# Scan decays, copies of B and small products in one ring of PSUM banks

## The chip, the cores and the metric

The kernel runs on one core of a Trainium2 chip. The metric is the device time of one execution in microseconds (us). The engines are named as in the profile: PE multiplies matrices (PEld is its loading of weights), DVE is the vector engine, ACT the scalar engine with the activation functions, POOL the GpSimd engine, and SP issues the DMAs. PSUM is the memory that PE writes its products to;[...] DVE and ACT read and write it too.

## The reference

Two layers work on four images of 48 x 48 tokens and 128 channels. The first normalises, projects, convolves (3 x 3, depthwise) and then runs a selective scan over the 2304 tokens in four directions `k` (by rows, by columns, and both reversed), for 256 channels with 16 states each:

```python
dt = softplus(dts + dt_proj_b)
A = -exp(A_logs).reshape(K, d, N)

def step(h, inp):
    dt_l, u_l, B_l, C_l = inp
    dA = exp(dt_l[..., None] * A)
    h = h * dA + (dt_l * u_l)[..., None] * B_l[:, :, None, :]
    y = einsum('bkdn,bkn->bkd', h, C_l)
    return h, y
```

The second layer is attention over the tokens, and then an STU: a causal convolution of the tokens with 16 spectral filters (`phi`), each followed by a projection with its own matrix, mixed over four lengths. Every layer adds to its input.

## The kernel before

**Stages.** The images follow one another. Each has a scan stage and then a stage of epilogue and attention. The scan stage runs beside matrix work that is independent of it: in image 0 `mixture` (products that mix the STU's matrices, into `gd` in DRAM), in images 1 to 3 the STU of the image before (`stu`). The STU of image 3 runs alone at the end.

**The scan stage.** A direction is cut into six chunks of `CS` = 384 tokens, so that an image has 24 chunks. A chunk has eight units `(h, q)`: a half `h` of the channels and a quarter `q` of the states. A unit works on a tile `s` of 128 partitions (32 channels by 4 states) by `G4` = 4 groups by 385 columns. Its life is:

- `spread` (L442): ACT copies the row of B, spread over the partitions (`bc`, in SBUF), into a PSUM bank (L445). Only for units whose multiply is on DVE.
- `enter` (L447): `s` = (dt u) times B in one multiply over 4 x 384 columns (L453). In three of eight units, the `POOLED` ones, POOL does it from `bc`; in five DVE does it from the copy.
- `decay` (L455), once for each group: ACT writes `exp(A dt)` (L459) into a PSUM bank `dA`. For group 0 it first copies the carried state into a spare column of `s` (L458).
- `scan` (L462), once for each group: DVE's `tensor_tensor_scan` (L465) runs over `s` with the decay as its factor.
- `times_c` (L468): POOL multiplies `s` by C (L474). `sum_c` (L476): PE sums the states into a bank `y` (L482). `add_y` (L485): DVE adds `y` to the image's sum (L488).

**Small products.** For the chunks ahead, `Chunk.prep` (L344) makes dt: a product `xp` (L370; only for `k` < 2, the other two directions read it from DRAM) that ACT copies to `xd` (L375), two products `dt` (L382) that ACT copies to `re` (L385), a softplus on ACT (L393), a multiply on DVE (L411), and a way through DRAM into the tiles `rep`, from which the units read. `prep` is a generator of three pieces for each unit's time. `mm_tile` hands its products a bank.

**The order of the work** is written out by hand in `scans` (L516), and each engine runs its own instructions in that order. Step `s` of its loop enters unit `s + 1` (POOL: `s + 2`), then takes the four scans of unit `s`, with a piece of `prep` before the first, before the third and after it; `spread(s + 2)` comes ahead of the third scan. Between the scans `more` advances the matrix work, by columns of PE's work, so that it ends with the scans. ACT's part of the matrix work falls between its decays: in `stu` a product `cx` (L1006) is copied to the bank `cy` (L1022), so that a second product may add to it, and then to `U` (L1029, L1030); the other one from `cy` to `U` (L1026). PE's next product on the same bank waits for these copies. In `mixture` they are the copies `Gm` (L829) and the scaled identities `W` (L839, L840).

**The PSUM banks of a scan stage**, eight in all: three for decays (`psa`; decay `i` takes bank `i` mod 3, and is issued just ahead of scan `i - 2`), one named B for the copies of B and the small products (`psB`), one for `y` (`psy`), two for `stu` or `mixture` (`psc`), one for the STU's projections (`psp`, which stays unused in image 0).

```python
        def scan(s, g):
            i = G4 * s + g
            decay(i + len(dAs) - 1)
            units[s].scan(g, dAs[i % len(dAs)])
```

Of the kernel before, what the change touches and what calls it, by code (L numbers as in the profile page):

```python
# [8 lines left out]
F32 = mybir.dt.float32  # L9
AF = mybir.ActivationFunctionType  # L10
ALU = mybir.AluOpType
AX = mybir.AxisListType
PSUM = bass.MemoryType.PSUM
DRAM = bass.MemoryType.DRAM

P = 128
B, H, W, C = 4, 48, 48, 128
# [4 lines left out]
CS = 384  # L22
SUB = 384
NT = L // P
G4, DL, C4, Q4 = 4, 32, 4, 4
# [30 lines left out]
def hybrid_kernel(ctx: ExitStack, tc: tile.TileContext, a: dict, out: bass.AP):  # L56
# [3 lines left out]
    nc = tc.nc  # L60
# [5 lines left out]
    bank = {}  # L66
# [246 lines left out]
    def in_order(t, k, lo, n):  # L313
# [2 lines left out]
            return t[:, lo // W:(lo + n) // W, :]  # L316
        return t.rearrange("p h w -> p w h")[:, lo // H:(lo + n) // H, :]

    def mm_tile(name):
        pool, tag = bank["mm"]  # L320
        return pool.tile([P, 512], F32, tag=tag, name=name)

    class Chunk:


        def __init__(self, b, k, c):
            self.b, self.k, self.lo = b, k, c * CS
            self.name = f"{b}_{k}_{c}"
            self.bc, self.rep = {}, []
            self.rev = k >= 2  # L330
            self.first = c == (NCH - 1 if self.rev else 0)
            self.last = c == (0 if self.rev else NCH - 1)

            self.slot = CS if self.rev else 0
            self.at = slice(0, CS) if self.rev else slice(1, CS + 1)

        def scanned(self, g):

            lo, n = g * (CS + 1), CS + 1
            if self.rev:  # L340
                return slice(lo + n - 1, lo - 1 if lo else None, -1)
            return slice(lo, lo + n)

        def prep(self, pool):  # L344

            k, name, xc = self.k, self.name, xcs[self.b]  # L350
            xdd_ = xdd[k % 2][self.lo // CS]

            def rest(n=1):

                yield
                yield 0
                yield
                for i in range(3 * n - 3):
                    yield 0 if i % 3 == 1 else None

            if k >= 2:
                xd = self.xd = pool.xd.tile([P, CS], F32, tag="xd", name=f"xd{name}")
                nc.sync.dma_start(xd, xdd_)
            yield from rest(2)
            yield
            if k < 2:
                xd = self.xd = pool.xd.tile([P, CS], F32, tag="xd", name=f"xd{name}")
                ps = mm_tile(f"xp{name}")
                for h in range(NH):
                    nc.tensor.matmul(ps[:, :CS], xw[:, h, k, :], in_order(xc[h], k, self.lo, CS),  # L370
                                     start=(h == 0), stop=(h == NH - 1))
            yield 2 * CS if k < 2 else 0
            yield
            if k < 2:
                nc.scalar.activation(xd, ps[:, :CS], AF.Identity, bias=onerow)  # L375
            yield from rest()

            re = pool.one.tile([P, NH, 2, CS], F32, tag="re", name=f"re{name}")
            for h in range(NH):
                yield  # L380
                ps = mm_tile(f"dt{name}_{h}")
                nc.tensor.matmul(ps[:, :CS], dtw[:, k, h * P:(h + 1) * P], xd, start=True, stop=True)  # L382
                yield CS
                yield
                nc.scalar.copy(re[:, h, 0], ps[:, :CS])  # L385
                if h == 0:
                    if k < 2:
                        nc.sync.dma_start(xdd_, xd)
                    yield from rest()
            yield  # L390
            yield 0

            nc.scalar.activation(re[:, :, 0], re[:, :, 0], AF.Softplus)  # L393
            yield
            yield
            yield 0
            d = dram.tile([NH, G4, DL, 2, CS], F32, tag="dtdu", name=f"dtdud{name}")

            def store(h):
                nc.sync.dma_start(d[h].rearrange("g j i t -> (g j) i t"), re[:, h])  # L400

            def load(h):
                rep = pool.rep.tile([P, G4, 2, CS], F32, tag="rep", name=f"rep{name}_{h}")
                for c in range(C4):
                    nc.sync.dma_start(rep[c::C4], d[h].rearrange("g j i t -> j g i t"))
                self.rep.append(rep)

            for h in range(NH):
                x = in_order(xc[h], k, self.lo, CS)
                dt, dx = [re[:, h, i].rearrange("p (r w) -> p r w", w=x.shape[2]) for i in range(2)]  # L410
                nc.vector.tensor_tensor(dx, dt, x, ALU.mult)  # L411
            yield
            yield
            store(0)
            yield 0
            store(1)
            yield
            yield from rest(2)
            load(0)
            yield from rest(2)  # L420
            yield
            yield 0
            load(1)
            yield
# [9 lines left out]
    class Unit:  # L434


        def __init__(self, ch, h, q):
            self.ch, self.h, self.q = ch, h, q
            self.name = f"{ch.name}_{h}_{q}"
            self.pool = (h, q) in POOLED  # L440

        def spread(self, ps):  # L442

            self.bt = ps.tile([P, 512], F32, tag="B", name=f"B{self.name}")
            nc.scalar.copy(self.bt[:, :CS], self.ch.bc[self.q])  # L445

        def enter(self, pool):  # L447

            full = self.full = pool.tile([P, G4, CS + 1], F32, tag="s", name=f"s{self.name}")
            s = self.s = full[:, :, self.ch.at]  # L450
            bt = self.ch.bc[self.q] if self.pool else self.bt[:, :CS]
            eng = nc.gpsimd if self.pool else nc.vector
            eng.tensor_tensor(s, self.ch.rep[self.h][:, :, 1], bt.unsqueeze(1).to_broadcast([P, G4, CS]), ALU.mult)  # L453

        def decay(self, g, dA):  # L455
            ch = self.ch
            if g == 0:
                nc.scalar.copy(self.full[:, :, ch.slot], none if ch.first else carry[:, self.h, self.q])  # L458
            nc.scalar.activation(dA[:, 1:CS + 1], ch.rep[self.h][:, g, 0], AF.Exp,  # L459
                                 scale=A[:, ch.k, self.h * G4 + g, self.q:self.q + 1])  # L460

        def scan(self, g, dA):  # L462
            ch = self.ch
            s = self.full.rearrange("p g t -> p (g t)")[:, ch.scanned(g)]
            nc.vector.tensor_tensor_scan(s, dA[:, CS + 1:0:-1] if ch.rev else dA[:, :CS + 1], s, 0.0,  # L465
                                         ALU.mult, ALU.add)

        def times_c(self):  # L468

# [43 lines left out]
            next(preps[2])  # L513
        yield chunks, preps

    def scans(b, chunks, preps, front, sp, back, work, work_cols):  # L516

        units = [Unit(ch, h, q) for ch in chunks for h, q in quads]
        total = len(chunks) * CHUNK_COLS + work_cols
# [10 lines left out]
        def enter(s):  # L530

            if s + 2 < len(units) and units[s + 2].pool:
                units[s + 2].enter(sp.s)
            if 0 <= s + 1 < len(units) and not units[s + 1].pool:
                units[s + 1].enter(sp.s)

        def decay(i):
            if i < G4 * len(units):
                units[i // G4].decay(i % G4, dAs[i % len(dAs)])

        def scan(s, g):
            i = G4 * s + g
            decay(i + len(dAs) - 1)
            units[s].scan(g, dAs[i % len(dAs)])

        def spread(s):
            if s < len(units) and not units[s].pool:
                units[s].spread(back.psB)

        def prepare(s):  # L550

# [10 lines left out]
                    nxt.fetch(i + u.q, front)  # L562

        pending = []
        dAs = [back.psa.tile([P, 512], F32, tag=f"dA{i}", name=f"dA{b}_{i}") for i in range(3)]
        for t in dAs:
            nc.vector.memset(t[:, 0:CS + 2:CS + 1], 0.0)
        spread(0)
        enter(-2)
        enter(-1)  # L570
        spread(1)
        for i in range(len(dAs) - 1):
            decay(i)
        for s in range(len(units) + 2):
            real = s < len(units)
            enter(s)
# [573 lines left out]
    def stu_alone(b, ps, seeds):  # L1150
        pool = Stage(tc, f"s{b}", "right", one=(1, SB), two=(2, SB), three=(3, SB), four=(4, SB))
        yield from stu(b, pool, ps, seeds)
        pool.close()
# [11 lines left out]
    start_y(0)  # L1165
    for b in range(B):
        sp = Stage(tc, f"h{b}", "left", s=(6, SB))
        ps = Stage(tc, f"b{b}", "right", psa=(1, PSUM), psy=(1, PSUM), psB=(1, PSUM), psc=(1, PSUM), psp=(1, PSUM))
        bank["mm"] = ps.psB, "B"
        if b == 0:  # L1170
            mixed = Stage(tc, "m", "right", two=(2, SB))
            scans(b, *first, front, sp, ps, mixture(mixed, ps), MIX_COLS)
            mixed.close()
        else:
            scans(b, *first, front, sp, ps, stu_alone(b - 1, ps, 1), STU_COLS)
        ps.close()
        sp.close()
        front.close()
# [20 lines left out]
        left = len(parts)  # L1199
# [75 lines left out]
```

## Time and profile before

| | |
|---|---|
| time, median of 3 runs | 5896.95 us (5894.11 to 5902.28) |
| profiled execution: its own time | 5896.91 us |
| its span, first to last instruction | 5895.2 us |
| granted PE clock, mean | 0.908 |
| scan stages, us from the span's start | 122 to 1092, 1382 to 2389, 2680 to 3682, 3973 to 4976 |
| a decay (L459), 3072 of them | 0.583 us |
| a scan (L465), 3072 | 0.942 us |
| a DVE multiply (L453), 480 | 1.734 us |
| a POOL multiply (L453), 288; (L474), 768 | 3.448 us; 3.178 us |

How to read it: a row of instructions gives line, engine, operation, `out<-in` by the program's names, the shape and the count, then the busy time in us and the mean in ns; after the second bar the idle time of the engine just before these instructions, and who ended most of it. A row of waits gives who waited for whom, then the total in us, how often, and the longest. A row of windows gives the stretch and its length, then for each engine the busy time and the number of instructions, the granted PE clock, the mean share of time that the DMA engines were busy, and GB/s. A row of the timeline gives start and length in us, engine, line, operation and names; in brackets the idle time before it and who ended it.

### The profile page before, as it was taken

The numbers are of one execution on the slowest core, as the hardware profiler recorded it, in microseconds if no ns is written. First come the engines' busy times: TensorE is split into PE (matmuls) and PEld (weight loads), VectorE is DVE, ScalarE is ACT, GpSimd is POOL, SyncE is SP. The second block draws the span as 40 slices with busy tenths as digits, with TensorE's granted clock in tenths as the row PEclk, the third lists the DMA queues.
The fourth block names the chain that finished last, engine by engine and source line by source line (L and its number), as shares of the span: only waits on it lengthen the run. The fifth ranks groups of instructions, "written<-read, shape, count | busy, mean of one in ns | idle before, by whom it ended". The sixth has DMA issues, their size and how long they took to land.

```text
span 5895.2 us, 74156 instructions
## 1 busy us (share of the span) xinstructions
PE 4906.8 (83%) x23826; PEld 3132.6 (53%) x23826; DVE 4268.4 (72%) x4926; ACT 3296.5 (56%) x6909; POOL 3620.1 (61%) x1823
## 2 busy tenths in 40 slices
PE   3555555597999998797999998779999998889999
PEld 1111111344566667545566666536666666468889
DVE  6999999756899998457999998548999997200000
ACT  2666666346777775246767765247777764332111
POOL 1999889504888998306888998107889987000000
PEclk6776777698999999898999999889999999999999
DMA  3444545206777778126877787127877876045546
GB/s 107 156 160 153 165 154 161 70 31 191 227 248 249 256 249 272 53 69 194 240 242 251 252 263 244 36 76 222 237 246 252 256 260 204 14 112 155 160 146 208
DMA packets 750565, 1066.87 MB, mean 181 GB/s; under 512 B 158528, under 2 KB 561088, under 8 KB 750144
## 3 DMA queue, kind: packets, MB, share of 16 engines
q1 hardware_dynamic: 744352, 1058.83, 57.6%
q10 hardware_dynamic: 5824, 3.30, 0.3%
q8 instruction: 190, 3.11, 0.2%
q14 instruction: 199, 1.63, 0.1%
HBM read 943.80 MB, written 117.98 MB: 180 GB/s over the span
## 4 chain that ended last, share of the span: by engine, by line
PE 45%; DVE 23%; DMA 11%; ACT 8%; POOL 5%; issue 4%; SPq 4%; ACTq 0%; DVEq 0%; POOLq 0%
PE cx L1006 15%; DVE s L465 11%; PE cy L1006 7%; PE pr L1069 5%; DVE s L453 5%; PE s L733 4%; PE y L482 4%; DMA rep<-dtdud 3%; PE o L726 3%; POOL s L474 3%; DMA tt<-fd 2%; SPq L432 2%; DVE xc L262 2%; ACT dA L459 2%; DMA bc<-xdd 2%
## 5 line engine op out<-in xcount | busy, mean ns | idle before, releaser
L465 DVE TENSOR_TENSOR_SCAN s<-dA,s 128x385 f32<-128x385 f32 x3072 | 2713.8, 942 | 217.6 <-ACT dA L459 216.5
L474 POOL TENSOR_TENSOR s<-s,bc 128x1536 f32<-128x1536 f32 x768 | 2438.9, 3178 | 131.6 <-DVE s L465 77.2
L459 ACT ACTIVATE dA<-rep,A 128x384 f32<-128x384 f32 x3072 | 1751.8, 583 | 801.0 <-DVE s L465 755.8
L453 POOL TENSOR_TENSOR s<-rep,bc 128x1536 f32<-128x1536 f32 x288 | 993.1, 3448 | 129.9 <-DMA bc<-xdd 119.6
L453 DVE TENSOR_TENSOR s<-rep,B 128x1536 f32<-128x1536 f32 x480 | 832.3, 1734 | 51.7 <-ACT B L445 26.2
L1006 PE MATMUL cx<-tt,us 128*128 128x254 f32 (+7 forms) x3840 | 815.4, 355 | 60.5 <-ACT U L1030 33.1
L1006 PE MATMUL cx<-tt,u 128*128 128x254 f32 (+7 forms) x3840 | 807.5, 353 | 48.4 <-ACT cy L1022 46.7
L1006 PE MATMUL cy<-tt,u 128*128 128x252 f32 (+5 forms) x3840 | 799.1, 352 | 39.8 <-DMA tt<-fd 39.8
L482 PE MATMUL y<-s,csum 128*32 128x384 f32 x6144 | 711.2, 537 | 140.2 <-POOL s L474 82.3
L1006 PEld LDWEIGHTS cx<-tt,u 128*128 128x128 f32 x3840 | 638.6, 190 | 295.7 <-issue 105.4
L1006 PEld LDWEIGHTS cx<-tt,us 128*128 128x128 f32 x3840 | 643.9, 192 | 255.8 <-issue 83.7
L1006 PEld LDWEIGHTS cy<-tt,u 128*128 128x128 f32 x3840 | 650.6, 193 | 187.8 <-issue 125.8
L1069 PE MATMUL pr<-U,G 128*128 128x288 f32 (+6 forms) x2048 | 593.2, 422 | 16.9 <-DMA G<-gd 16.7
L1096 DVE TENSOR_TENSOR res<-res,ot 126x512 f32<-126x512 f32 (+1 forms) x20 | 13.4, 671 | 687.1 <-PE ot L1090 687.1
L849 PE MATMUL G<-M,W 128*128 128x256 f32 (+3 forms) x512 | 244.4, 595 | 231.9 <-DMA M<-in_M_phi_plus 158.0
L1069 PEld LDWEIGHTS pr<-U,G 128*128 128x128 f32 x2048 | 342.8, 192 | 170.0 <-issue 94.9
L735 ACT ACTIVATE e<-s,shift 128x512 f32<-128x512 f32 (+1 forms) x360 | 230.8, 643 | 330.8 <-PE s L733 330.2
L156 POOL TENSOR_TENSOR ln_vu<-ln_vu,mhalf 128x4 f32<-128x4 f32 (+1 forms) x20 | 21.8, 1091 | 627.0 <-DVE ln_vu L155 627.0
L733 PE MATMUL s<-xnT 128*128 128x512 f32 (+1 forms) x720 | 357.2, 581 | 45.8 <-ACT xnT L695 23.3
L482 PEld LDWEIGHTS y<-s,csum 128*32 128x32 f32 x6144 | 126.9, 112 | 503.1 <-issue 286.6
L1029 ACT COPY U<-cx 128x252 f32<-128x252 f32 (+1 forms) x320 | 111.4, 348 | 420.3 <-PE cx L1006 420.1
L726 PE MATMUL o<-e,xn 128*128 128x512 f32 (+1 forms) x720 | 342.0, 558 | 4.5 <-ACT e L735 4.5
(161 smaller groups left out, 4016.4 us busy)
## 6 DMA issues: line engine op xcount, KB each, us to landing
rep<-dtdud SPq DMA_DIRECT2D x768, 384.0 KB
bc<-xdd SPq DMA_DIRECT2D x3072, 48.0 KB
tt<-fd SPq DMA_DIRECT2D x192, 577.0 KB
tt<-fd SPq DMA_DIRECT2D x192, 505.0 KB
dtdud<-re SPq DMA_DIRECT2D x192, 384.0 KB
tt<-fd SPq DMA_DIRECT2D x192, 379.0 KB
G<-gd SPq DMA_DIRECT2D x192, 256.0 KB
tt<-fd SPq DMA_DIRECT2D x64, 506.0 KB
```

The lines of the kernel that those rows point to most:

```text
L262: nc.vector.scalar_tensor_tensor(xc[h], x, cw[:, h, t:t + 1], xc[h], ALU.mult, ALU.add)
L453: eng.tensor_tensor(s, self.ch.rep[self.h][:, :, 1], bt.unsqueeze(1).to_broadcast([P, G4, CS]), ALU.mult)
L459: nc.scalar.activation(dA[:, 1:CS + 1], ch.rep[self.h][:, g, 0], AF.Exp, scale=A[:, ch.k, self.h * G4 + g, self.q:self.q + 1])
L465: nc.vector.tensor_tensor_scan(s, dA[:, CS + 1:0:-1] if ch.rev else dA[:, :CS + 1], s, 0.0, ALU.mult, ALU.add)
L474: nc.gpsimd.tensor_tensor(self.s, self.s, ch.bc[Q4 + self.q].unsqueeze(1).to_broadcast([P, G4, CS]), ALU.mult)
L482: nc.tensor.matmul(ch.y[g * DL:(g + 1) * DL, :CS], csum, self.s[:, g], start=(self.q == 0), stop=(self.q == Q4 - 1))
L726: nc.tensor.matmul(po[J][:, :w], xn[:, i], e[:, :w], start=(i == 0), stop=(i == NT - 1))
L733: nc.tensor.matmul(p[:, :w], xnT[:, i * P:(i + 1) * P], xnT[:, 512 * J:512 * J + w], start=True, stop=True)
L735: nc.scalar.activation(e[:, :w], p[:, :w], AF.Exp, bias=shift)
L849: nc.tensor.matmul(p[:, :n], W[:, q if t else 0, i], M[t][:, i].unsqueeze(1).to_broadcast([P, n, C]), start=(t == 0 and i == 0), stop=(t = ...
L1006: nc.tensor.matmul(p4[:, 1:3, v - (hi - at):] if g else p4[:, 0:4:3, v - (hi - at):], x, t[:, :, hi - 1 - at + J * P:end if end >= 0 else ...
L1069: nc.tensor.matmul(o if q else o.rearrange("p f r m -> p r f m"), G, U[n][:, 4 * q:4 * q + 4, v0:v1].rearrange("p (a b) m -> p a b m", a=2 ...
```

## The change

The banks `psa` and `psB` become one `Ring`: four banks, and five in image 0, where `psp` stood unused. Each bank is a tile of its own for the whole stage, with a zero in column 0 and in column 385, set once; decays, copies of B and products take columns 1 to 384. A list `free` holds the banks in the order in which the program gives them back, and `take` hands out the first one. What gives a bank back: a scan (its decay's), a multiply on DVE (B's), and ACT's copy of a small product.

`fill` runs ahead of each scan: first it spreads a wanted B, if a bank is free, and then issues decays as long as banks are free. So decays have no fixed distance to the scans any more. `spread(s + 2)` only puts the unit on the list `wanted`. `mm_hold` takes a bank one piece of `prep` ahead of the product, and `mm_done` returns it after ACT's copy. Outside scan stages `mm_hold` and `mm_done` do nothing.

```diff
+    class Ring:
+        def __init__(self, pool, n, name):
+            self.t = [pool.tile([P, 512], F32, tag=f"ring{i}", name=f"{name}_{i}") for i in range(n)]
+            for t in self.t:
+                nc.vector.memset(t[:, 0:CS + 2:CS + 1], 0.0)
+            self.free = list(range(n))
+            self.held = []
+        def take(self):
+            return self.free.pop(0)
+        def body(self, i):
+            return self.t[i][:, 1:CS + 1]
+        def decays(self, i, rev):
+            return self.t[i][:, CS + 1:0:-1] if rev else self.t[i][:, :CS + 1]
+
+    def mm_hold():
+        if isinstance(bank["mm"], Ring):
+            bank["mm"].held.append(bank["mm"].take())
+
     def mm_tile(name):
+        if isinstance(bank["mm"], Ring):
+            return bank["mm"].body(bank["mm"].held[0])
         pool, tag = bank["mm"]
         return pool.tile([P, 512], F32, tag=tag, name=name)
+
+    def mm_done():
+        if isinstance(bank["mm"], Ring):
+            bank["mm"].free.append(bank["mm"].held.pop(0))
...
             yield from rest(2)
+            if k < 2:
+                mm_hold()
             yield
...
                 nc.scalar.activation(xd, ps[:, :CS], AF.Identity, bias=onerow)
+                mm_done()
...
             for h in range(NH):
+                mm_hold()
                 yield
...
                 nc.scalar.copy(re[:, h, 0], ps[:, :CS])
+                mm_done()
...
-        def spread(self, ps):
-            self.bt = ps.tile([P, 512], F32, tag="B", name=f"B{self.name}")
-            nc.scalar.copy(self.bt[:, :CS], self.ch.bc[self.q])
+        def spread(self, ring):
+            self.bt = ring.take()
+            nc.scalar.copy(ring.body(self.bt), self.ch.bc[self.q])
...
             eng.tensor_tensor(s, self.ch.rep[self.h][:, :, 1], bt.unsqueeze(1).to_broadcast([P, G4, CS]), ALU.mult)
+            if not self.pool:
+                ring.free.append(self.bt)
...
-            nc.scalar.activation(dA[:, 1:CS + 1], ch.rep[self.h][:, g, 0], AF.Exp,
+            self.dA[g] = ring.take()
+            nc.scalar.activation(ring.body(self.dA[g]), ch.rep[self.h][:, g, 0], AF.Exp,
                                  scale=A[:, ch.k, self.h * G4 + g, self.q:self.q + 1])
...
-            nc.vector.tensor_tensor_scan(s, dA[:, CS + 1:0:-1] if ch.rev else dA[:, :CS + 1], s, 0.0,
-                                         ALU.mult, ALU.add)
+            i = self.dA.pop(g)
+            nc.vector.tensor_tensor_scan(s, ring.decays(i, ch.rev), s, 0.0, ALU.mult, ALU.add)
+            ring.free.append(i)
...
+        wanted, issued = [], [0]
+        def fill(left=0):
+            while wanted and ring.free:
+                wanted.pop(0).spread(ring)
+            while len(ring.free) > left and issued[0] < G4 * len(units):
+                i = issued[0]
+                issued[0] += 1
+                units[i // G4].decay(i % G4, ring)
+
         def scan(s, g):
-            i = G4 * s + g
-            decay(i + len(dAs) - 1)
-            units[s].scan(g, dAs[i % len(dAs)])
+            fill()
+            units[s].scan(g, ring)
 
         def spread(s):
             if s < len(units) and not units[s].pool:
-                units[s].spread(back.psB)
+                wanted.append(units[s])
...
         spread(0)
+        fill(len(ring.free) - 1)
         enter(-2)
         enter(-1)
         spread(1)
-        for i in range(len(dAs) - 1):
-            decay(i)
+        fill(1)
...
-        ps = Stage(tc, f"b{b}", "right", psa=(1, PSUM), psy=(1, PSUM), psB=(1, PSUM), psc=(1, PSUM), psp=(1, PSUM))
-        bank["mm"] = ps.psB, "B"
+        ps = Stage(tc, f"b{b}", "right", psa=(1, PSUM), psy=(1, PSUM), psc=(1, PSUM), psp=(1, PSUM))
+        ring = bank["mm"] = Ring(ps.psa, 4 if b else 5, f"ring{b}")
```

More of the change, by code (lines that the diff above doesn't have):

```diff
@@ L335, in __init__ @@
             self.at = slice(0, CS) if self.rev else slice(1, CS + 1)
[L337 to L342, printed above, removed]
         def prep(self, pool):
@@ L440, in __init__, with enter, decay @@
             self.pool = (h, q) in POOLED
-        def spread(self, ps):
-            self.bt = ps.tile([P, 512], F32, tag="B", name=f"B{self.name}")
-            nc.scalar.copy(self.bt[:, :CS], self.ch.bc[self.q])
-        def enter(self, pool):
+            self.dA = {}
+        def spread(self, ring):
+            self.bt = ring.take()
+            nc.scalar.copy(ring.body(self.bt), self.ch.bc[self.q])
+        def enter(self, pool, ring):
             full = self.full = pool.tile([P, G4, CS + 1], F32, tag="s", name=f"s{self.name}")
             s = self.s = full[:, :, self.ch.at]
-            bt = self.ch.bc[self.q] if self.pool else self.bt[:, :CS]
+            bt = self.ch.bc[self.q] if self.pool else ring.body(self.bt)
             eng = nc.gpsimd if self.pool else nc.vector
             eng.tensor_tensor(s, self.ch.rep[self.h][:, :, 1], bt.unsqueeze(1).to_broadcast([P, G4, CS]), ALU.mult)
-        def decay(self, g, dA):
+            if not self.pool:
+                ring.free.append(self.bt)
+        def decay(self, g, ring):
             ch = self.ch
@@ L458, in decay, with scan @@
                 nc.scalar.copy(self.full[:, :, ch.slot], none if ch.first else carry[:, self.h, self.q])
-            nc.scalar.activation(dA[:, 1:CS + 1], ch.rep[self.h][:, g, 0], AF.Exp,
+            self.dA[g] = ring.take()
+            nc.scalar.activation(ring.body(self.dA[g]), ch.rep[self.h][:, g, 0], AF.Exp,
                                  scale=A[:, ch.k, self.h * G4 + g, self.q:self.q + 1])
-        def scan(self, g, dA):
+        def scan(self, g, ring):
             ch = self.ch
-            s = self.full.rearrange("p g t -> p (g t)")[:, ch.scanned(g)]
-            nc.vector.tensor_tensor_scan(s, dA[:, CS + 1:0:-1] if ch.rev else dA[:, :CS + 1], s, 0.0,
-                                         ALU.mult, ALU.add)
+            s = self.full[:, g, ::-1 if ch.rev else 1]
+            i = self.dA.pop(g)
+            nc.vector.tensor_tensor_scan(s, ring.decays(i, ch.rev), s, 0.0, ALU.mult, ALU.add)
+            ring.free.append(i)
         def times_c(self):
@@ L514, in begin_scans, with scans @@
         yield chunks, preps
-    def scans(b, chunks, preps, front, sp, back, work, work_cols):
+    def scans(b, chunks, preps, front, sp, back, ring, work, work_cols):
         units = [Unit(ch, h, q) for ch in chunks for h, q in quads]
@@ L532, in enter @@
             if s + 2 < len(units) and units[s + 2].pool:
-                units[s + 2].enter(sp.s)
+                units[s + 2].enter(sp.s, ring)
             if 0 <= s + 1 < len(units) and not units[s + 1].pool:
[L535 to L539, printed above, removed]
+                units[s + 1].enter(sp.s, ring)
+        wanted, issued = [], [0]
[6 more added lines that the diff above has]
+                units[i // G4].decay(i % G4, ring)
         def scan(s, g):
-            i = G4 * s + g
-            decay(i + len(dAs) - 1)
-            units[s].scan(g, dAs[i % len(dAs)])
+            fill()
+            units[s].scan(g, ring)
         def spread(s):
             if s < len(units) and not units[s].pool:
-                units[s].spread(back.psB)
+                wanted.append(units[s])
         def prepare(s):
@@ L564, in scans @@
         pending = []
-        dAs = [back.psa.tile([P, 512], F32, tag=f"dA{i}", name=f"dA{b}_{i}") for i in range(3)]
-        for t in dAs:
-            nc.vector.memset(t[:, 0:CS + 2:CS + 1], 0.0)
         spread(0)
+        fill(len(ring.free) - 1)
         enter(-2)
@@ L1167, in hybrid_kernel @@
         sp = Stage(tc, f"h{b}", "left", s=(6, SB))
-        ps = Stage(tc, f"b{b}", "right", psa=(1, PSUM), psy=(1, PSUM), psB=(1, PSUM), psc=(1, PSUM), psp=(1, PSUM))
-        bank["mm"] = ps.psB, "B"
+        ps = Stage(tc, f"b{b}", "right", psa=(1, PSUM), psy=(1, PSUM), psc=(1, PSUM), psp=(1, PSUM))
+        ring = bank["mm"] = Ring(ps.psa, 4 if b else 5, f"ring{b}")
         if b == 0:
             mixed = Stage(tc, "m", "right", two=(2, SB))
-            scans(b, *first, front, sp, ps, mixture(mixed, ps), MIX_COLS)
+            scans(b, *first, front, sp, ps, ring, mixture(mixed, ps), MIX_COLS)
             mixed.close()
         else:
-            scans(b, *first, front, sp, ps, stu_alone(b - 1, ps, 1), STU_COLS)
+            scans(b, *first, front, sp, ps, ring, stu_alone(b - 1, ps, 1), STU_COLS)
         ps.close()
```

## The prediction

> **What bounds the kernel now.** I read the page's engine line, then the windows of the four scan stages, then the waits inside them, and last a stretch of the timeline.
>
> ```profile
> PE 4906.8 (83%) x23826; PEld 3132.6 (53%) x23826; DVE 4268.4 (72%) x4926; ACT 3296.5 (56%) x6909; POOL 3620.1 (61%) x1823
> ...
> L465 DVE TENSOR_TENSOR_SCAN s<-dA,s 128x385 f32<-128x385 f32 x3072 | 2713.8, 942 | 217.6 <-ACT dA L459 216.5
> L459 ACT ACTIVATE dA<-rep,A 128x384 f32<-128x384 f32 x3072 | 1751.8, 583 | 801.0 <-DVE s L465 755.8
> L453 DVE TENSOR_TENSOR s<-rep,B 128x1536 f32<-128x1536 f32 x480 | 832.3, 1734 | 51.7 <-ACT B L445 26.2
> ```
>
> The scans sit idle 217 us before starting, nearly all for a decay that ACT has not written; ACT in turn waits 756 us for a scan to give a bank back. 217 us (3.7%) is the most that a deeper supply of decays could return, if nothing else bounded the stages.
>
> ```profile
> core 0: us, PE busy (x) PEld busy (x) DVE busy (x) ACT busy (x) POOL busy (x), PEclk, DMA share, GB/s
> 122.00:1092.00 970.00, 516.54 (x2160) 164.88 (x2160) 919.70 (x978) 644.03 (x1357) 872.02 (x423) 0.72 0.49 157
> 1382.00:2389.00 1007.00, 936.62 (x5112) 633.35 (x5116) 921.88 (x983) 704.34 (x1521) 871.83 (x423) 0.97 0.78 244
> ```
>
> Image 0 is DVE's stage (920 of 970 us busy), with POOL (872) close behind. In image 1 (images 2 and 3 read the same, 1002 and 1003 us long) PE is busy 937 and DVE 922 of 1007. Shorter windows show that they take turns: from 1560 to 1760 PE is busy 190.2 of 200 us and DVE 184.4; from 2000 to 2200 it is 190.2 and 192.5. So early in an image PE sets the pace and DVE's waits are its symptom; later DVE does.
>
> Waits of image 1 (1382 to 2389), DVE, PE and ACT:
>
> ```profile
> DVE s L465 <- ACT dA L459: 65.7, 57, 5.4
> DVE s L453 <- ACT B L445: 6.6, 6, 2.0
> ...
> PE cx L1006 <- ACT cy L1022: 14.1, 17, 1.5
> PE cx L1006 <- ACT U L1030: 10.9, 8, 2.6
> ...
> PE xp L370 <- DVE s L453: 5.9, 4, 2.7
> PE dt L382 <- DVE s L453: 5.9, 10, 0.9
> ...
> ACT dA L459 <- DVE s L465: 156.3, 181, 1.9
> ACT U L1029 <- PE cx L1006: 51.7, 40, 4.9
> ```
>
> PE never waits for a scan directly. It waits for copies that ACT owes it (25 us), and for the DVE multiply that holds bank B (12 us). Why ACT owes them:
>
> ```profile
> 2095.70 0.58 ACT L459 ACTIVATE dA<-rep,A 128x384 f32<-128x384 f32 x1 [1.93 <-DVE s L465]
> 2096.22 0.53 ACT L1022 COPY cy<-cx 128x504 f32<-128x504 f32 x1
> ...
> 2096.80 3.64 PE L1006 MATMUL cx<-tt,u 128*128 128x252 f32 x16 [1.52 <-ACT cy L1022]
> ```
>
> ACT stood 1.93 us in front of a decay whose bank was not free; the copy behind it came late, and PE idled 1.52 us. Any wait that the change puts on ACT is paid in this way.
>
> **What the Trainium skill says.** "Perfetto Trace Analysis", Optimization Strategy: the same gap repeating on the engine that should be saturated can mean too little PSUM for the next tile. The 217 us agree in kind. "PSUM — Partial Sum Buffer", Engine vs sequencer instructions: ScalarE's queue is strict FIFO; the excerpt above shows it. "ScalarE: Activation LUTs", What ACT_TABLE_LOAD costs: about 1283 ns a load; the trace shows 1.283 us in all 22 loads at L393 of image 1, so a softplus with a load on either side holds ACT for 1.28+0.84+1.28 = 3.4 us.
>
> **The change, part by part.** PE, DVE, POOL and SP's queue keep their order, so no DMA moves on any queue; only ACT's order differs, with the same instructions. Five more memsets, 17 for 12, of 0.07 us lie ahead of the first multiply, which waits for its copy anyway (5.89 us in image 0): nothing; without that cover, 0.35 us.
>
> 1. Depth. Before, a decay is issued two scans ahead, always. After, each image's ring gives up one bank for B from the fill at a unit's third scan to the next multiply (5 of 8 units: 10 of a chunk's 32 fills), and one for each small product during a whole unit (3 of 8: 12 fills, 8 where `xd` comes from DRAM). With four banks, a third decay stands ahead in only 10 to 14 of 32. With five (image 0) it stands ahead throughout, sometimes a fourth.
>
> 2. What that saves in images 1 to 3. I followed the 162 waits of scans for decays (193 us) back along ACT's rows. 78 us lie behind the softplus and its loads, 115 us behind copies that had themselves waited for PE (L1022, L1026, L1029). The softplus falls where B holds the fourth bank: the same decays stand ahead of it as before; B's copy (about 0.47) only takes the place of a decay (0.58) in front of it, 0.1 us each, 22 an image: 2 us. Of the copies about half get one more decay ahead, worth at most one scan (0.94) each: 27 us in three images, 9 each. Sum 11 us of DVE an image; about half of it lies where DVE sets the pace: **-5.5**.
>
> 3. The products. `dt` and `xp` no longer wait for the multiply but for the scan ahead of it, 1.73 us earlier; the waits of up to 0.9 and 2.7 us go: 12 us of PE an image. What is late next is the copy L1022.
>
> 4. The added wait. At a unit's first scan a ring fill issues a decay into the bank that the multiply just gave back. ACT then waits for the multiply's end where it waited for the scan before: 1.73 us later, in the five of eight units with a DVE multiply there. Behind it on ACT stand the copies cx to cy (L1022) and to U (L1029, L1030), for which PE waits. A quarter of 80 copies of each kind times 5/8 is 12 an image of each. Bounds: nothing where PE is itself late (ACT waited 52 us for it at L1029), and 2 x 12 x (1.73+0.58) = 55 us if PE had no slack at all. Set on the trace one by one, each against the matmul that needs it, they give 28 us in three images: 9 us of PE an image. I take that. With step 3 PE gains 12-9 = 3 us, half where PE sets the pace: **-1.5**. The products' decay (the unit's third) also waits for the multiply, but has 1.9 us of scans ahead of it and needs 0.65: nothing; at 0.15 us for each of 66 it would be 10 us an image.
>
> B's copy now waits for a scan with two scans (1.88 us) until its multiply, and takes 0.47 plus a hand-over: it stays hidden unless a copy ahead of it waits for PE, as now (6.6 us).
>
> 5. Image 0. Waits there:
>
> ```profile
> DVE s L465 <- ACT dA L459: 23.5, 19, 10.1
> DVE ya L488 <- PE y L482: 20.7, 11, 3.9
> ...
> PE dt L382 <- DVE s L453: 82.4, 32, 5.1
> ...
> PE xp L370 <- DVE s L453: 44.9, 7, 9.1
> ```
>
> One wait of 10.1 is a late load of M and shortens by 0.94; the other 18 average 0.74, under one scan, and go: 14 us. Of the y waits none to all 20.7 may go, since PE stops waiting for bank B; but `y` also waits for POOL's product (60.3 us), so I count none. POOL may keep a little: **-13**.
>
> Sum: 3 x (-5.5-1.5) - 13 = -34; I round images 1 to 3 down to -5 each, since freed waits there meet the other engine: -15-13 = **-28 us**. The profiled execution took 5896.91 us (span 5895.2), level with the median of 5896.95, so the forecast is 5869.
>
> **Rivals.** *ACT pays for the multiply* (slower): step 4 runs at twice the one-by-one count (PE +19 an image, all on the path) and the third decay costs its 10: 3 x (19+10-12-5) - 10 = +26, 5923. It decides once ACT's added lateness exceeds PE's slack before L1006, as at 2096.80. For: PE at 93%, no slack to hide in; ACT already 156 us an image behind scans. Against: where PE is bound, ACT is mostly early.
> *The two sides cancel* (no change): -13 in image 0 becomes -5, and images 1 to 3 give nothing, because the ring's fourth bank is lent out in most fills, so that it hardly deepens anything: 5892.
> *All decays ready* (far faster): scans never wait, and PE, with its own waits for DMA (22 us), floors a stage at about 960: 3 x -43 - 23 = -152, 5745. The softplus argument of step 2 speaks against it.
>
> **How the numbers follow.** A measurement here tells about 0.2%, 12 us, from no change. Chances: modest gain around 5869, 0.44; cancelling, 0.25; slower, 0.28; far faster, 0.03. The gain case spans -12 to -62 (all of y's 20.7, and 7 an image more); the cancelling case crosses the bound of 12 a little on the slow side. Faster 0.47, same 0.23, slower 0.30. The slow case has no sharp end (55 us an image is its bound in step 4), so the range, 5833 to 5938, passes its value by 15 us, and leaves out its tail and the far gain.
>
> **What would show it.** After: softplus waits of scans stay in images 1 to 3 (DVE on decays near 50 us each, from 64), and fall below 12 us in image 0; `dt` and `xp` no longer wait for L453; PE's wait for cy and L1030 rises from 25 to about 34 us an image; ACT's waits name the multiply. I am wrong if stages of images 1 to 3 lengthen, if decay waits fall under 25 us, or if waits for B grow past 15 us an image.

## The result, and the profile after

| | before | after |
|---|---|---|
| time, median of 6 runs | 5893.63 us (5887.60 to 5902.28) | 5873.84 us (5868.63 to 5888.05) |
| ratio, 95% interval | | 0.9968 (0.9955 to 0.9981) |
| profiled execution, its span | 5895.2 us | 5875.7 us |
| image 0, first to last scan | 969.8 us | 970.8 us |
| images 1, 2, 3 | 1005.8, 1001.5, 1002.6 us | 999.5, 992.9, 998.9 us |

The change saves 20 us, 0.3% (11 to 27 us by the interval). The forecast was 28 us (5869). But the time came from elsewhere than forecast: in the profiled executions image 0, from which 13 us were expected, gave nothing (+1), and images 1 to 3 gave 18.6 in place of 15.

The costliest groups that answer to those shown of before, from the page after. What was `dA` and `B` is now `ring`:

```profile
L497 DVE TENSOR_TENSOR_SCAN s<-ring,s 128x385 f32<-128x385 f32 x3072 | 2706.4, 939 | 120.7 <-ACT ring L490 118.9
...
L490 ACT ACTIVATE ring<-rep,A 128x384 f32<-128x384 f32 x3072 | 1759.6, 584 | 816.8 <-DVE s L481 461.6
...
L481 DVE TENSOR_TENSOR s<-rep,ring 128x1536 f32<-128x1536 f32 x480 | 831.5, 1733 | 72.9 <-ACT ring L473 28.2
```

The scans' waits for decays fell by 98 us, from 217 to 119; the time fell by 20. ACT waits in front of decays as long as before (817 us, from 801), but now more than half of it for a multiply (L481, 462 us). The waits of image 1, DVE's, PE's and ACT's, first the one of before that the prediction does not show, then those of after:

```profile
DVE ya L488 <- PE y L482: 4.4, 8, 0.9
```

```profile
DVE s L497 <- ACT ring L490: 33.6, 36, 2.6
DVE ya L520 <- PE y L514: 19.8, 9, 7.3
...
DVE s L481 <- ACT ring L473: 5.3, 2, 5.2
...
PE cx L1041 <- ACT cy L1057: 21.3, 16, 3.6
PE cx L1041 <- ACT U L1065: 17.0, 10, 2.9
...
PE ring L394 <- DVE s L497: 0.5, 1, 0.5
...
ACT ring L490 <- DVE s L481: 109.7, 87, 1.9
ACT ring L490 <- DVE s L497: 63.9, 153, 3.8
ACT U L1064 <- PE cx L1041: 42.7, 41, 3.8
```

Three things moved. DVE's wait for decays halved (66 to 34), but its wait for PE's sums `y` rose from 4 to 20: a part of what DVE gained in one place it lost in another. The products (L394, L408) no longer hold PE up: 12 us became 0.5. And PE waits longer for ACT's copies to cy and U, 38 us where it was 25. One such wait in the timeline after:

```profile
2171.72 0.59 ACT L490 ACTIVATE ring<-rep,A 128x384 f32<-128x384 f32 x1
...
2172.41 1.73 DVE L481 TENSOR_TENSOR s<-rep,ring 128x1536 f32<-128x1536 f32 x1
2172.53 0.58 ACT L490 ACTIVATE ring<-rep,A 128x384 f32<-128x384 f32 x1 [0.23 <-DVE s L497]
...
2174.18 0.58 ACT L490 ACTIVATE ring<-rep,A 128x384 f32<-128x384 f32 x1 [1.06 <-DVE s L481]
...
2174.70 0.35 ACT L1057 COPY cy<-cx 128x288 f32<-128x288 f32 x1
...
2175.10 3.20 PE L1041 MATMUL cx<-tt,u 128*128 128x144 f32 x12 [3.62 <-ACT cy L1057]
```

The multiply ends at 2174.14; the decay that was issued into its bank starts 0.04 us later; the copy behind that decay comes after it, and PE had been idle for 3.62 us. ACT's wait for the multiply is 1.06 us of them; the three decays that ACT ran meanwhile are another 1.75.

Image 0 after, waits of DVE and PE:

```profile
DVE ya L520 <- PE y L514: 25.4, 12, 4.9
DVE s L497 <- ACT ring L490: 12.9, 3, 10.3
...
PE G L884 <- DMA M<-in_M_phi_plus: 141.1, 13, 33.8
...
PE G L884 <- ACT Gm L864: 74.2, 15, 10.5
```

The decay waits are gone but for one of 10.3 us behind the late load of M, much as forecast (12.9 us are left, under 12 were named). DVE waits for `y` and for the multiply instead (25 and 12 us, before: 21 and 7), and is idle for 50 us in all, as before.

### The profile page after: what moved, and what is told of

The parts are those of the page before. It is cut to its first block, busy times and chain, and to the rows that moved or that the text cites. A ratio compares the mean times of both kernels' runs of the same rounds, so it can differ in the third digit from the quotient of the medians.

```text
span 5875.7 us, 73876 instructions
## 1 busy us (share of the span) xinstructions
PE 4903.8 (83%) x23826; PEld 3137.6 (53%) x23826; DVE 4281.4 (73%) x4931; ACT 3310.1 (56%) x6909; POOL 3621.0 (62%) x1823
## 5 line engine op out<-in xcount | busy, mean ns | idle before, releaser
L497 DVE TENSOR_TENSOR_SCAN s<-ring,s 128x385 f32<-128x385 f32 x3072 | 2706.4, 939 | 120.7 <-ACT ring L490 118.9
L490 ACT ACTIVATE ring<-rep,A 128x384 f32<-128x384 f32 x3072 | 1759.6, 584 | 816.8 <-DVE s L481 461.6
L481 POOL TENSOR_TENSOR s<-rep,bc 128x1536 f32<-128x1536 f32 x288 | 994.0, 3451 | 137.5 <-DMA bc<-xdd 132.1
L481 DVE TENSOR_TENSOR s<-rep,ring 128x1536 f32<-128x1536 f32 x480 | 831.5, 1733 | 72.9 <-ACT ring L473 28.2
L1131 DVE TENSOR_TENSOR res<-res,ot 126x512 f32<-126x512 f32 (+1 forms) x20 | 13.4, 671 | 687.1 <-PE ot L1125 687.1
```

The lines of the kernel that those rows point to most:

```text
L490: nc.scalar.activation(ring.body(self.dA[g]), ch.rep[self.h][:, g, 0], AF.Exp, scale=A[:, ch.k, self.h * G4 + g, self.q:self.q + 1])
L497: nc.vector.tensor_tensor_scan(s, ring.decays(i, ch.rev), s, 0.0, ALU.mult, ALU.add)
```

## The experiments

Ratios are to the kernel before, timed beside each variant on the same chip. The stages are those of images 0 to 3, from first to last scan, in one profiled execution each. The changed kernel and the one of run 7 have the same program in images 1 to 3, and yet differ by 10 us in the sum of these three stages (2991.3 and 3001.2), so smaller differences of such sums are not read below. "Greedy fill" is the `fill` of the changed kernel, which issues decays as long as banks are free.

**1. Banks rotate, order unchanged (depth2).**

```diff
-        def fill(left=0):
+        def fill(left=0, upto=1):
...
-            while len(ring.free) > left and issued[0] < G4 * len(units):
+            while len(ring.free) > left and issued[0] <= min(upto, G4 * len(units) - 1):
...
-            fill()
+            fill(0, G4 * s + g + 2)
```

> The ring as in the changed kernel, but a decay is issued at most two scans ahead, so that every engine's order is that of the kernel before, and only the banks rotate: products and copies of B take the bank that has been free longest. If the extra decay makes the gain (theory): 0.999 to 1.001 of before less the products' part, about 5888 us, with scans waiting 60 us an image for decays as before. If the products' earlier bank makes it (rival): about 5874 us, and dt and xp no longer wait for the multiply in both cases.

Measured: 5850.72 us, 0.9916 (0.9903 to 0.9929), faster than the changed kernel by 0.5%, the intervals apart. Stages: 956.4, and 998.9, 988.8, 996.0. In the traces ACT's 6909 instructions stand in the same order as in the kernel before, and DVE's differ by the five memsets alone. The theory of the prediction fell here. It said that the additional decay ahead is the gain. Without it the kernel is 50 us faster than before, and with it only 20. So the change is two things of opposite sign: other banks, worth some 50 us, and the greedy fill, which costs some 30 by the ratios (22 in the profiled stages, 14 of them in image 0). In images 1 to 3 the ring has no more banks than before had for the same users (four: three and B), so there it is the choice of the bank alone; in image 0 a fifth bank comes with it (run 7). Image 1's waits in depth2:

```profile
DVE s L497 <- ACT ring L490: 56.3, 46, 6.0
...
DVE ya L520 <- PE y L514: 1.9, 3, 0.7
...
PE cx L1041 <- ACT cy L1057: 13.2, 13, 2.5
PE cx L1041 <- ACT U L1065: 9.8, 7, 2.6
...
ACT ring L490 <- DVE s L481: 94.9, 83, 1.9
ACT ring L490 <- DVE s L497: 66.7, 154, 3.6
```

The scans wait more for decays (56 us, after: 34), yet the stage is no longer: PE is held up less (23 us for copies, after: 38) and `y` is on time. ACT's own wait for DVE is no smaller (162 us, before 156), so it isn't that ACT stands less; it stands elsewhere.

**2. One decay ahead (depth1).** The same with `G4 * s + g + 1`.

> The ring with a decay issued one scan ahead at most: ACT's copies for PE come ahead of one decay more, and each decay's bank is older still. If what counts is that ACT's copies for PE do not stand behind decays (theory): 5840 to 5855 us, PE's wait for cy and U under 21 us an image. If the scans need the second decay ready when ACT waits for PE or loads tables (rival): scans wait over 100 us an image for decays, 5900 us or more.

Measured: 5868.74 us, 0.9949 (0.9935 to 0.9962). Neither: PE's wait for copies did fall to 18.9 us in image 1 (9.8 + 9.1), but the scans' wait for decays rose to 77.7. The stages are 956.0, and 999.6, 995.4, 998.9; image 0 is as short as in depth2. With the same banks one, two and as many decays as possible ahead give 0.9949, 0.9916, 0.9968: two is best.

**3. Which bank a decay takes (depth2_newest).** The edit is made in depth2:

```diff
-            self.dA[g] = ring.take()
+            self.dA[g] = ring.free.pop()
```

> depth2 with one difference: a decay takes the bank that was given back last, while products and copies of B still take the oldest. Every engine's order is still that of the kernel before. If depth2 is fast because a decay's bank was freed long ago, so that ACT need not stand in front of it (theory): most of the gain goes, 5880 to 5895 us, and scans wait 60 us or more an image for decays. If it is fast because products and B no longer share one bank (rival): 5850 us as depth2.

Measured: 5895.99 us, 0.9996 (0.9987 to 1.0004). The whole gain of depth2 goes with the choice of the bank, at the same order on every engine. The newest bank at a unit's first scan is the multiply's; ACT's waits in image 1:

```profile
ACT ring L490 <- DVE s L481: 143.4, 88, 4.4
```

In the kernel before a decay never waited for the multiply. So this isn't a pure return to before: products keep their earlier bank here, and decays wait for a later event than they did. That these two cancel is likely, not shown by this run; run 4 prices the products apart.

**4. Which bank a product takes (depth2_holdlast).** The edit is made in depth2:

```diff
-            bank["mm"].held.append(bank["mm"].take())
+            bank["mm"].held.append(bank["mm"].free.pop())
```

> depth2, but a small product takes the bank given back last, the multiply's, so that dt and xp wait for the multiply as in the kernel before; decays and copies of B still take the oldest bank, and every engine's order is still that of the kernel before. If depth2's gain is in the decays' older banks (theory): 5850 to 5862 us. If it is in the products' bank (rival, which depth2_newest leaves open, since its decays wait for the multiply): 5880 us or more.

Measured: 5879.14 us, 0.9967 (0.9955 to 0.9979); stages 955.3, and 1002.5, 997.8, 1002.0. It fell on the rival's edge. PE waits 14 us again in image 1 for the multiply (L394, L408), and images 1 to 3 lose most of what they had (18.6 us together), image 0 nothing. So in depth2 some 30 us (0.9967 to 0.9916) belong to products that take the bank free longest, in images 1 to 3, and the other 20 to what is left: the banks of decays and of the copies of B, and in image 0, where most of it lies, the fifth bank. These three were not tested apart.

**5. The same edit in the changed kernel (holdlast).**

> A small product takes the bank that was given back last (the multiply's), so the decay of that unit's third scan waits for a scan again and not for the multiply; dt and xp wait for the multiply as before. Theory (the products' bank is worth 1 to 2 us an image, the decay's wait nothing): 5874 to 5880 us, waits of dt and xp back at 12 us of PE an image. Rival (ACT's wait for the multiply costs what PE pays): faster, about 5865 us, and PE's wait for the copies to cy and U falls from 38 us an image towards 30.

Measured: 5887.44 us, 0.9983 (0.9976 to 0.9989), about 9 us worse than the changed kernel by the ratios, though the intervals overlap; stages 966.1, and 1001.3, 995.8, 1006.5. The rival's gain did not come: PE's wait for the copies was still 36 us in image 1, and freeing the third scan's decay from the multiply made nothing faster. That the products' bank is worth more than the 1 to 2 us an image of the theory is likely from this run, and clear with two decays ahead (run 4).

**6. No ACT instruction waits for the multiply early (late).**

```diff
+            self.later = []
...
-                ring.free.append(self.bt)
+                ring.later.append(self.bt)
...
-            bank["mm"].held.append(bank["mm"].take())
+            r = bank["mm"]
+            r.held.append(r.later.pop() if r.later else r.take())
...
             fill()
+            ring.free += ring.later
+            ring.later.clear()
```

> A multiply's bank goes to a product where one is wanted, and otherwise back to the ring only after the next fill, so no ACT instruction ahead of a unit's second scan waits for the multiply. If ACT's wait for the multiply costs PE 9 to 13 us an image on the path (step 4 as predicted): faster than the changed kernel, 5855 to 5865 us, and PE's wait for cy and U back at 25 us an image. If these waits fall where PE has slack (rival): no faster, 5874 to 5882 us, since a decay fewer stands ahead.

Measured: 5880.23 us, 0.9967 (0.9955 to 0.9979), level with the changed kernel; stages 967.5, and 998.8, 995.4, 1002.6. PE's waits in image 1 in this kernel:

```profile
PE cx L1045 <- ACT cy L1061: 15.7, 17, 1.5
...
PE cx L1045 <- ACT U L1069: 10.6, 8, 2.5
...
PE ring L410 <- DVE s L483: 5.4, 10, 0.7
```

The copies are back at 26 us. `late` takes two things from in front of them at once, ACT's wait for the multiply at a unit's first scan and the decay that had waited. depth2_newest tells whether the wait alone can do it: that kernel has no decay more in front than the kernel before, only the waits for the multiply, and PE waits 39 us for the copies there (19.6 + 19.2), against 23 in depth2. So that wait is enough to raise them to 38. But in `late` the products wait for the multiply again and one decay fewer stands ahead, and the sum is the same, as the rival said. What step 4's 13 us cost at the end can't be read from this run alone.

**7. Four banks in image 0 (four0).** `Ring(ps.psa, 4, ...)` throughout.

> Four banks in image 0 too, images 1 to 3 unchanged. If image 0 is held by the product y and by POOL, not by decays (theory): image 0's stage stays within 3 us of 970, total 5874 us. If the fifth bank pays for something that the y waits hide (rival): image 0 grows by 5 to 15 us, total about 5884 us.

Measured: 5882.84 us, 0.9974 (0.9964 to 0.9983), within the interval of the changed kernel; image 0 took 974.1 us. With the greedy fill the fifth bank is worth 3 us in the two profiles, between theory and rival. What it is worth with two decays ahead was not tested.

**8. No table loads (exp_before, exp_after).** `AF.Softplus` became `AF.Exp` in both kernels, which leaves out the softplus.

> The kernel before with Exp in place of Softplus (dt is another number; the kernel no longer needs two table loads, 2.57 us of ACT, around each of 24 softplus an image). Theory: of the 64 us an image that scans wait for decays, some 26 lie behind the softplus and go; about half of them on the path: 40 to 60 us less in all, about 5845 us. Rival (scans wait for PE anyway): under 15 us less.

> The changed kernel with Exp in place of Softplus (dt is another number). Theory: the decay waits that are left in images 1 to 3 (34 to 37 us each) lie behind the softplus, where the ring has no spare bank; they fall under 12 us an image, and the gain is the same as in the kernel before with the same edit, so the ring's 20 us stay: about 5825 us. Rival (ring and softplus cure the same waits): the two kernels with Exp are within 6 us of each other.

Measured: 5839.31 us, 0.9911 (0.9898 to 0.9925), and 5834.85 us, 0.9904 (0.9891 to 0.9918). The size for the kernel before was as expected, and for the pair the rival's outcome came: without the table loads the ring makes no measurable difference. Image 1, DVE's waits, first the kernel before with Exp, then the changed kernel with Exp:

```profile
DVE s L465 <- ACT dA L459: 36.6, 32, 6.5
DVE ya L488 <- PE y L482: 6.1, 6, 1.5
```

```profile
DVE ya L520 <- PE y L514: 19.3, 11, 6.8
DVE s L497 <- ACT ring L490: 15.6, 21, 5.0
```

But the rival's reason, that ring and softplus cure the same waits, does not hold. The ring again takes 21 us of decay waits away, and 13 come back at `y`, the rest at the multiply. DVE is idle for 56.0 and 57.7 us in image 1.

**9. M one round earlier (mahead_before, mahead_after).** In `mixture`:

```diff
+        Ms = {}
+
+        def load_M(k):
+            if k < KF:
+                Ms[k] = [pool.two.tile([P, NF, C], F32, tag=f"M{j}", name=f"M{j}_{k}") for j in range(2)]
+                for t, src in zip(Ms[k], ("M_phi_plus", "M_phi_minus")):
+                    nc.sync.dma_start(t, a[src][:, k].rearrange("i d e -> d i e"))
+
+        load_M(0)
         for k in range(KF):
-            M = [pool.two.tile([P, NF, C], F32, tag=f"M{j}", name=f"M{j}_{k}") for j in range(2)]
-            for t, src in zip(M, ("M_phi_plus", "M_phi_minus")):
-                nc.sync.dma_start(t, a[src][:, k].rearrange("i d e -> d i e"))
+            load_M(k + 1)
+            M = Ms.pop(k)
```

> The kernel before, with the loads of M issued one round of the mixture earlier, which touches image 0 alone. Theory: PE no longer stands 7 to 13 us in front of a product G, y is on time, DVE's 21 us of waits for y fall under 8: image 0 10 to 20 us shorter, about 5880 us. Rival (POOL holds image 0): under 4 us.

> The changed kernel with the same earlier loads of M. Theory: y was what took the place of the decay waits in image 0 (25 us of DVE), so image 0 now shows the ring's gain as well: 8 to 15 us shorter than the kernel before with the same edit, in all about 5850 us. Rival (POOL or the multiply holds image 0): image 0 as long as in the kernel before with this edit, about 5862 us.

Measured: 5874.97 us, 0.9969 (0.9962 to 0.9975), and 5855.93 us, 0.9941 (0.9927 to 0.9954). The late M did cause the waits for `y`: before, they fall from 20.7 to 4.8 us, and image 0 from 969.8 to 953.0. But image 0 of the changed kernel becomes 952.9: the ring adds nothing there even when `y` is on time. The rival's outcome came, but not for its reason: run 10 shortens image 0 further with the same work on POOL and the same multiplies. The gap of 19 us between the two comes from images 1 to 3 (995.0, 995.5, 1002.1 against 1005.8, 1002.1, 1003.2).

**10. The two together (depth2_mahead).**

> depth2 with the loads of M issued one round earlier. If depth2's shorter image 0 and the earlier loads cure different waits: 5850 - 19 = 5831 us, image 0 near 945. If both cure the late y of image 0 (rival; two kernels with M early had image 0 at 953): image 0 stays at 950 to 953, total about 5847 us.

Measured: 5840.19 us, 0.9899 (0.9885 to 0.9912), the fastest kernel of this study with the whole computation; it beats both. Image 0 took 945.5 us. Its window, and DVE's waits in it:

```profile
122.00:1068.00 946.00, 535.79 (x2160) 169.44 (x2160) 930.02 (x978) 649.34 (x1357) 872.41 (x423) 0.73 0.51 161
```

```profile
DVE s L497 <- ACT ring L490: 14.0, 4, 10.0
DVE ya L520 <- PE y L514: 6.1, 2, 5.5
```

DVE is busy 930 of 946 us, and one wait of 10 us, behind the first M, is most of the rest. With M early and two decays ahead, almost nothing but DVE's own time is left in image 0 (of which the last section shows a part to be drawn out); with M early and the greedy fill it still took 7 us more.

## Why the prediction was right, and where it was wrong

**The number** lay within the range and on the forecast's side: 20 us for 28. That it came so near is luck. Of the 34 us before rounding, 29.5 were for decays that stand further ahead (16.5 in images 1 to 3, 13 in image 0), and issuing further ahead costs some 30; only 4.5, the products' worth less the wait that ACT takes on, were for other banks, which bring some 50. The two errors offset each other.

**Steps 1 and 2 (depth) had the wrong sign.** They took the additional decay as the gain. depth2 shows that issuing further ahead costs. What they mis-sized besides can be followed back by one rule in both kernels: from a waiting scan along ACT's rows to ACT's last idle time over 0.15 us, where a table load met on the way counts the wait as the softplus's. In images 1 to 3 this gives 102 us behind the softplus and 91 behind copies before, and 79 and 27 after; the split of 78 and 115 in the prediction does not come out of the trace by this rule. So the softplus's part did not stay: it fell by 23 us where 6 were forecast, and it does so in depth2 too (79), by the banks alone. Behind copies 27 us were to go, and 64 went, though by ACT's order only 450 of the 1280 copies for PE in these images, not half, have a decay more ahead of them than before. Even so most of that did not reach the end: in image 1 DVE's total idle time fell by 11 us (84.6 to 73.8), not by 32, because `y` and the multiply were late next. The prediction named "the other engine" only as a reason to round down.

**Step 3 (products) was too small.** It read their worth from PE's wait alone, 12 us an image, set 9 against it, and counted half. The waits went as said. Giving them back costs about 9 us in all with the greedy fill and 30 with two decays ahead. ACT's copies of the products come earlier too, and nothing in the step counted what is queued behind them; that this is the reason is argued, not shown.

**Step 4 (ACT waits for the multiply) was right in mechanism and near in size:** PE's waits for copies rose by 13 us in image 1, 9 were forecast, and `late` and depth2_newest show the cause. That `late` isn't faster is left open above.

**Step 5 (image 0) failed:** -13 forecast, +1 measured. The decay waits went, as it said, and `y` was counted at none in either direction; it rose by 5 us, the multiply's waits by 5 too. The kernels with M early show that a late `y` is not all of it, since they are level with `y` on time in both. depth2 shows what took the gain: the same five banks without the greedy fill give 13.4 us. So in image 0 the fill costs about what the banks bring. The likely way is the mixture's copies (Gm, W), which by ACT's order in the traces stand behind one or two decays more than before. PE's wait for Gm was 74 us after, 66 before and 56 in depth2; with M early its waits for Gm and W together are 157 us with the greedy fill, 140 in the kernel before and 115 with two decays ahead. Which of ACT's copies it is, and how it reaches the scans, was not separated.

**The rivals.** "The two sides cancel" was right for image 0, with another reason than it gave. "ACT pays for the multiply" has its mechanism shown and its weight not. The far gain did not appear; the end of the gain case, 62 us, is a sum that comes to 70 with the terms that are named for it, which changes nothing here. Of what would show it: the scans' waits for decays in images 1 to 3 ended at 34 to 37 us an image rather than 50; the products stopped waiting for the multiply; PE's waits reached 38 rather than 34; ACT's waits name the multiply.

**Open** is why the age of a decay's bank is worth so much while ACT's total wait for DVE hardly differs (156 us before, 162 in depth2, 174 after, in image 1).

## What to carry to other kernels

Pooling buffers does two things: each user gets the buffer that has been free longest, and work can be issued earlier. Test them apart: here the first was worth 50 us and the second cost 30. One way in which it costs was seen: ACT runs its instructions in the program's order, so one that is issued into a buffer just given back puts its wait ahead of everything behind it (PE waited 38 us for copies in image 1, with two decays ahead 23). Whether that is all of the 30 was not shown. Before counting a wait as gained, name the next one that the same engine will meet; 98 us of waits for decays went here, and 20 us of time.

## What was not expected of the hardware

The multiplies of `re` (L411 before, L438 after; 128x384, median 0.80 and 0.81 us) took up to 1.77 us in image 1 of the kernel before, but up to 3.41 us after and 3.21 in depth2. The longest one after, the first of the two DVE multiplies in the second row, beside POOL's multiply by C:

```profile
1722.73 3.17 POOL L506 TENSOR_TENSOR s<-s,bc 128x1536 f32<-128x1536 f32 x1
...
1723.16 4.14 DVE L438 TENSOR_TENSOR re<-re,xc 128x384 f32<-128x384 f32 x2
```

POOL's multiply ends at 1725.90, the first of the two on DVE at 1726.57. It is so throughout: of the 192 multiplies of `re` in each kernel, every one that started while a multiply by C ran on POOL (32 before, 44 after) ended 0.41 to 0.81 us after POOL's, and every other took at most 0.87 us. The scans and DVE's multiplies by B are not drawn out in this way (at most 1.01 and 1.78 us); they read an operand from PSUM, and the multiplies of `re` do not, but that this is the reason was not tested. More of them met POOL after the change, and this is most of why DVE was busy 4 us longer in each of images 1 to 3. In image 0 of run 10 the multiplies of `re` take 55 of DVE's 930 us, in the kernel before 41.
